# State sums turned through VectorE blocks and DRAM instead of TensorE, and the keys' quad issued next to the features' quad

## The chip, the cores and the metric

The kernel runs on one core of a Trainium2 chip. Its time is the device time of one execution in microseconds (us); a kernel's figure is the median of its runs. Besides the timed runs there is one execution under the hardware profiler, and every duration of a single instruction below comes from that one.

The engines are called as in the profile: PE is TensorE (PEld are its weight loads), DVE is VectorE, ACT is ScalarE, POOL is GpSimd, and SP is the engine that issues the DMAs. Every engine takes its instructions in the order in which they are written, and waits on semaphores for the others.

## The reference: linear attention with running sums, then a small mixture of experts

The input x is 2 x 2048 tokens of 256 channels, in float32. Cut to what matters here:

```python
h = layernorm(x) * (1 + ca) + sa
q, k, v = split(h @ W_attn + b_attn)                 # 16 heads of 16
phi(x) = exp(x @ omega - 0.5 * sum(x * x)) / sqrt(128)   # 128 features per head
S = cumsum(phi_k[..., :, None] * v[..., None, :])    # state: 128 x 16 per head
Z = cumsum(phi_k)                                    # 128 per head
y = (phi_q . S) / (phi_q . Z + 1e-6)
x = x + ga * (y @ W_proj + b_proj)
h = layernorm(x) * (1 + cb) + sb
x = x + gb * moe(h)          # 4 experts, the best 2 of a softmax; base 256 -> 1024 -> 256 and low rank of 4
```

The cumulative sums run over all 2048 tokens of a batch entry.

## The kernel before

**Blocks and steps.** The 4096 tokens are cut into 8 blocks `i` of 512 tokens (blocks 0 to 3 are the first batch entry). The 16 heads form 4 groups `g` of 4 heads, and the 512 tokens form 4 chunks `t` of 128, taken in two pairs `u`. One block therefore has 8 steps `k`, one for each (g, u): step k handles the pair (k // 2, k % 2). The main loop goes over 8 x 8 steps, n = 8 i + k.

**The attention part of one step.** Within a chunk, `scores` (L496) multiplies key and query features into two PSUM banks `pa`, and `masks` (L507, DVE) copies them to SBUF under a causal mask as `am`. Across chunks, the sums S and Z travel as a state: `increments` (L522) forms the chunk's addition, transposed as (heads and values) x features, in the first half of one PSUM bank `py_bank`, and DVE adds it to the running sum `ST` (L535). `turn_sums` (L542) turns two sums with two TensorE transposes, again in `py_bank`, and ACT copies them to SBUF as `S` (L548; DVE in a few early pairs). `outputs` multiplies `am` with the values (L562) and the features with the entering state S (L565), both into the second half of `py_bank`; ACT copies that to `y` (L571), and after each second pair SP stores y (L575).

**Features.** A "quad" is four matmuls with 32 rows each, one for every head of a group, which lie in four row groups of the PE array and run side by side. `features` (L452) is the quad for one side (queries or keys) of one group, followed by four exponentials on ACT (L463). `token_keys` (L478) is the second quad of the keys, with tokens on the partitions, followed by four exponentials (L483). `reload` (L420) loads the inputs of the features from DRAM.

**Dense work.** Each step begins with a share of the dense work (`dense`), so that PE has something to do while the others finish: in even steps query/key projections of the next block (L372), and besides these at k = 0 the turning of the normalized input (L337) and a part of `finish` (L776), at k = 2 `finish` and `project` (L619), at k = 4 `channels2`, `router` (L645), `choose` (some 25 small DVE instructions, L668 to L706) and `finish`, at k = 6 the values (L433). Odd steps hold a "unit" of the hidden layer: `hidden` (L740), then `first` (four low-rank matmuls L725 as a quad, and ACT's ReLU), and after `outputs` `second` (another quad L725, DVE's L767, POOL's L768). Block 1 has units only at k = 5 and 7, block 0 none. The attention part uses the banks `pa` and `py_bank`; all else shares five banks `mm`. In a step with a unit, three of the four features matmuls borrow `py_bank` and `pa` ("spare").

**Order.** `keep_written_order` fixes the order of the instructions on each engine to that in which the program was written; nothing is moved by a scheduler. One step is written in this order: `dense`, `turn_sums`, `first`, `token_keys` of the next group (even k), then for the next pair `increments`, `scores`, `masks` (the first two swapped in odd steps without a unit), then `outputs` of this pair, `second`, `features`, `load_more` (weights, in the first 13 steps), `amid` (at k = 0 the inverse of the denominators: L597 on DVE, then the store L599 and two loads L602 on SP; at k = 1 the division, L611; then `reload`), and `behind` (loads of x at k = 1). Dependencies on a PSUM bank are kept for the tile as a whole: in the profile `outputs` (L562, second half of `py_bank`) waits for DVE's sums (L535, which read the first half).

Of the kernel before, what the change touches and what calls it, by code (L numbers as in the profile page):

```python
# [9 lines left out]
FP = mybir.dt.float32  # L10
# [22 lines left out]
def kernel(  # L33
# [479 lines left out]
    def increments(i, g, u):  # L513

        kt = turned[i, g]
        for e in range(2):
            t = 2 * u + e
            if not carried(i, t):
                continue
            for j in range(HG):  # L520
                v0 = (t * NH + g * HG + j) * DV
                nc.tensor.matmul(  # L522
                    py_bank[j * HW : (j + 1) * HW, e * P : (e + 1) * P],
                    st[i]["vs"][:, v0 : v0 + HW], kt[:, j, t, :], start=True, stop=True,
                )
        for e in range(2):
            t = 2 * u + e
            if not carried(i, t):
                continue
            new = work.tile([P, M], FP, tag=f"ST{g}", name=f"ST{i}_{g}{t}")  # L530
            ps = py_bank[:, e * P : (e + 1) * P]
            if i % NBLK == 0 and t == 0:
                nc.vector.tensor_copy(new, ps)
            else:
                nc.vector.tensor_add(new, ps, S[g])  # L535
            S[g] = sums[i, g, t] = new

    def turn_sums(i, g, u):

        n = sum(carried(i, 2 * u + e) for e in range(2))  # L540
        for e in range(n):
            nc.tensor.transpose(  # L542
                py_bank[:, e * P : (e + 1) * P], sums.pop((i, g, 2 * u + e)), ident
            )
        s2 = work.tile([P, 2, P], FP, tag=f"S{g}", name=f"S{i}_{g}{u}")
        short = (i == 0 and (g, u) != (3, 0)) or (i == 1 and (g, u) in ((0, 0), (0, 1), (1, 1)))
        copy = nc.vector.tensor_copy if short else nc.scalar.copy
        copy(s2[:, 0:n].rearrange("p e d -> p (e d)"), py_bank[:, 0 : n * P])  # L548
        for e in range(n):
            state[i * NT + 2 * u + e + 1, g] = s2[:, e]  # L550

    def outputs(i, g, u):

# [2 lines left out]
        for e in range(2):  # L556
            t = 2 * u + e
            am, s0 = staged.pop((i, g, t)), state.pop((i * NT + t, g), None)
            py = bank[:, (2 + e) * P : (3 + e) * P]
            for j in range(HG):  # L560
                v = st[i]["v"][:, t, g * HG + j, :]
                nc.tensor.matmul(py[rows[j], :], v, am[:, j, :], start=True, stop=s0 is None)  # L562
            if s0 is not None:
                for j in range(HG):
                    nc.tensor.matmul(  # L565
                        py[rows[j], :], s0[:, rows[j]], phi[i, g, 0, j][:, t * P : (t + 1) * P],
                        start=False, stop=True,
                    )
        if u == 0:
# [368 lines left out]
    for i in range(N):  # L938
        for k in range(PAIRS):
# [2 lines left out]
            turn_sums(*pair_at(n))  # L942
            if unit_at(i, k):
                first(*unit_at(i, k))
            if k % 2 == 0 and n + 2 < TOTAL:
                token_keys(*pair_at(n + 2)[:2])
            if n + 1 < TOTAL:
                steps = [increments, scores]
                if k % 2 and not unit_at(i, k):
                    steps.reverse()  # L950
                for step in steps + [masks]:
                    step(*pair_at(n + 1))
# [3 lines left out]
                second(*unit)  # L956
            gi, gg, side = quad_at(n + 3)
            if gi < N:
                spare = [py_bank] + pa if unit else ()
                exponentials(*features(gi, gg, side, spare))  # L960
            load_more(i * PAIRS + k)
            amid(i, k)
            behind(i, k)

# [91 lines left out]
```

## Time and profile before

| what | before |
|---|---|
| median of 3 runs | 741.91 us (740.5 to 750.78) |
| profiled execution, its own time | 742.97 us |
| its span on the core | 741.2 us |
| granted TensorE clock | 0.998 |
| PE busy | 713.5 us (96%) |
| DVE, ACT, POOL busy | 377.5, 341.4, 150.5 us |
| queue that SP issues, share of 16 DMA engines | 29.8% |

The busy time of an engine is the sum over the stretches in which it worked; PE's ends are modelled, so that a busy PE may still be waiting for weights or for its array to empty. A timeline row gives the start, the time from the first start to the last end, the engine, the line, the operation, the tiles (written <- read), the shape, how often, and in brackets the idle time of the engine ahead of it with what ended it.

### The profile page before, as it was taken

What the parts mean: (1) busy time and instruction counts of PE and PEld (TensorE: products, weight loads), DVE (VectorE), ACT (ScalarE), POOL (GpSimd) and SP (SyncE); (2) the same over time, 40 slices, a digit from 0 to 9 for tenths busy, and PEclk for the clock granted to TensorE, in tenths of its full rate; (3) what the DMA queues carried; (4) which work ended last, traced back from release to release, by engine and by line L of the source; (5) the groups of instructions that cost most, each with busy time, mean ns of one, the idle gap of its engine ahead of it and who ended that gap; (6) DMA issues with size and microseconds to landing.
All of it is one profiled execution on the core that took longest, in us unless ns stands there. A gap on an engine that the chain in (4) does not pass through costs nothing.

```text
span 741.2 us, 25787 instructions
## 1 busy us (share of the span) xinstructions
PE 713.5 (96%) x11350; PEld 538.2 (73%) x11350; DVE 377.5 (51%) x1030; ACT 341.4 (46%) x678; POOL 150.5 (20%) x193
## 2 busy tenths in 40 slices
PE   7899898899999999999999999999999999999998
PEld 5466665677777778777777777777787777787776
DVE  5744757454664545564564546644555436522532
ACT  1556454555454554545454554445545554431020
POOL 2101403032321311131120312122101212114022
PEclk9999999999999999999999999999999999999999
DMA  5446456423412242332412243223313322011100
GB/s 149 144 120 183 132 155 178 144 73 99 136 58 88 76 142 63 101 88 89 145 35 89 69 133 101 73 74 90 116 45 101 88 64 85 19 56 47 49 24 29
DMA packets 47664, 69.51 MB, mean 94 GB/s; under 512 B 8320, under 2 KB 21824, under 8 KB 47552
## 3 DMA queue, kind: packets, MB, share of 16 engines
q1 hardware_dynamic: 45936, 66.81, 29.8%
q8 instruction: 89, 1.46, 0.8%
q10 hardware_dynamic: 1616, 1.05, 0.5%
q14 instruction: 23, 0.19, 0.1%
HBM read 38.20 MB, written 29.64 MB: 92 GB/s over the span
## 4 chain that ended last, share of the span: by engine, by line
PE 88%; DVE 6%; ACT 3%; DMA 2%; issue 1%; POOL 0%; SPq 0%; DVEq 0%
PE ph L740 15%; PE pf L776 12%; PE pa L496 8%; PE pq L372 7%; PE pp L452 7%; PE ph L725 5%; PE py_bank L522 4%; PE pk L478 4%; PE py_bank L562 4%; PE po L619 4%; PE py_bank L565 3%; PE pv L433 3%; ACT phi L463 2%; PE pf L799 2%; PE py_bank L542 2%; DMA inv<-rdr 1%
## 5 line engine op out<-in xcount | busy, mean ns | idle before, releaser
L768 POOL TENSOR_TENSOR g<-g,r 128x256 f32<-128x256 f32 x128 | 94.5, 771 | 419.8 <-DVE g L767 419.8
L463 ACT ACTIVATE phi<-pp,lnm 128x512 f32<-128x512 f32 x184 | 113.4, 688 | 52.7 <-PE pp L452 52.7
L740 PE MATMUL ph<-h,wi_sb 128*128 128x256 f32 x480 | 111.6, 386 | 0.0
L740 PEld LDWEIGHTS ph<-h,wi_sb 128*128 128x128 f32 x480 | 87.5, 189 | 32.4 <-ACT y L571 19.0
L776 PE MATMUL pf<-wo_g,g 128*128 128x256 f32 x448 | 103.3, 381 | 0.0
L776 PEld LDWEIGHTS pf<-wo_g,g 128*128 128x128 f32 x448 | 83.3, 190 | 17.0 <-issue 4.9
L535 DVE TENSOR_TENSOR ST<-py_bank,ST 128x128 f32<-128x128 f32 x112 | 32.6, 291 | 122.3 <-PE py_bank L522 94.3
L507 DVE TENSOR_TENSOR am<-pa,causal 128x512 f32<-128x512 f32 x128 | 82.8, 686 | 23.5 <-PE pa L496 22.6
L483 ACT ACTIVATE kt<-pk,lnm 128x512 f32<-128x512 f32 x128 | 77.6, 690 | 23.7 <-PE pk L478 23.7
L496 PE MATMUL pa<-phi,phi 128*32 128x64 f32 (+3 forms) x4096 | 86.3, 234 | 1.6 <-ACT phi L463 0.8
L496 PEld LDWEIGHTS pa<-phi,phi 128*32 128x32 f32 x4096 | 82.4, 110 | 4.3 <-ACT phi L463 3.3
L548 ACT COPY S<-py_bank 128x256 f32<-128x256 f32 (+1 forms) x54 | 19.2, 356 | 115.3 <-PE py_bank L542 115.3
L452 PE MATMUL pp<-f,om 32*128 32x512 f32 x368 | 70.2, 632 | 0.0
L372 PE MATMUL pq<-hT,w_sb 128*128 128x512 f32 x128 | 62.0, 608 | 2.6 <-DVE hT L340 1.6
L784 DVE SCALAR_TENSOR_TENSOR xt<-pf,wt,xt 128x256 f32<-128x256 f32 x32 | 15.4, 482 | 89.6 <-PE pf L776 78.5
L562 PE MATMUL py_bank<-am,v 128*17 128x128 f32 x1024 | 51.3, 273 | 9.1 <-DVE ST L535 8.0
L571 ACT COPY y<-py_bank 128x256 f32<-128x256 f32 x64 | 23.9, 373 | 62.8 <-PE py_bank L565 54.5
L767 DVE SCALAR_TENSOR_TENSOR g<-ph,rho 128x256 f32<-128x256 f32 x120 | 42.5, 417 | 19.8 <-PE ph L725 14.7
L565 PE MATMUL py_bank<-phi,S 128*17 128x128 f32 x960 | 49.5, 273 | 0.0
L372 PEld LDWEIGHTS pq<-hT,w_sb 128*128 128x128 f32 x128 | 22.2, 189 | 32.3 <-issue 15.9
L754 ACT ACTIVATE r<-ph 128x256 f32<-128x256 f32 x120 | 36.6, 389 | 18.4 <-PE ph L725 14.9
L725 PE MATMUL ph<-lT,lb_sb 16*128 16x256 f32 (+1 forms) x480 | 43.5, 425 | 0.7 <-ACT lT L719 0.7
(148 smaller groups left out, 936.1 us busy)
## 6 DMA issues: line engine op xcount, KB each, us to landing
qd<-qs SPq DMA_DIRECT2D x64, 256.0 KB
f<-qd SPq DMA_DIRECT2D x62, 256.0 KB
ydr<-y SPq DMA_DIRECT2D x32, 256.0 KB
num<-ydr SPq DMA_DIRECT2D x16, 256.0 KB
inv<-rdr SPq DMA_DIRECT2D x16, 256.0 KB
xt<-in_x_dram SPq DMA_DIRECT2D x8, 256.0 KB
xt<-in_x_dram SPq DMA_DIRECT2D x32, 64.0 KB
wo_g<-in_woT_dram SPq DMA_DIRECT2D x4, 512.0 KB
```

Of the source, the lines that this page charges most:

```text
L372: nc.tensor.matmul(pq, w_sb[:, k, n * P : (n + 1) * P], s["hT"][:, k, :], start=(k == 0), stop=(k == KC - 1),)
L452: nc.tensor.matmul(pp, om[rs, :], f[rs, :], start=True, stop=True, tile_position=(2 * DH * j, 0))
L463: nc.scalar.activation(ph, pps[j], AF.Exp, bias=lnm)
L483: nc.scalar.activation(kt[:, j].rearrange("p t m -> p (t m)"), banks[j], AF.Exp, bias=lnm)
L496: nc.tensor.matmul(pa[e][c * CG : (c + 1) * CG, j * P + q0 : j * P + q1], k[j][:, t0 + c * CG : t0 + (c + 1) * CG], q[j][:, t0 + q0 : t0 + ...
L507: nc.vector.tensor_mul(am, pa[e][:].rearrange("p (h q) -> p h q", h=HG), causal[:, e, :].unsqueeze(1).to_broadcast([P, HG, P]),)
L562: nc.tensor.matmul(py[rows[j], :], v, am[:, j, :], start=True, stop=s0 is None)
L565: nc.tensor.matmul(py[rows[j], :], s0[:, rows[j]], phi[i, g, 0, j][:, t * P : (t + 1) * P], start=False, stop=True,)
L725: nc.tensor.matmul(ph, lb_sb[rs, (f0 + j) * P : (f0 + j + 1) * P], s["lT"][rs, ts], start=False, stop=True, skip_group_check=True, tile_po ...
L740: nc.tensor.matmul(ph, wi_sb[:, k, f * P : (f + 1) * P], s["h2"][:, k, ts], start=(k == 0), stop=False, skip_group_check=True,)
L768: nc.gpsimd.tensor_add(g, g, r[j // 2][:, j % 2, :])
L776: nc.tensor.matmul(po, s["g"][f][:, t * P : (t + 1) * P], wo_g[i // NBLK][:, f, :], start=(f == 0), stop=(f == NF - 1), skip_group_check=True,
```

## The change

- In blocks 1 to 7 the sums are no longer turned by PE and copied by ACT. Behind the additions, and ahead of the masks, DVE turns each entering sum in 32x32 blocks (L546 of the changed kernel); SP stores the result to DRAM (`sd`) and, at the end of the step, loads it with four DMAs of 32 partitions into `S`, in an order that completes the transposition. `outputs` of the next step waits for these loads. The loads stand in SP's queue behind `load_more` and ahead of `amid`.
- Block 0 still turns on PE, but only the sums that enter (12 transposes remain of 120), and in the step that uses them.
- In an even step whose next step has a unit ("late": 25 steps with a keys' quad), `token_keys` moves from ahead of `increments` to behind `outputs`, right ahead of `features`, which then borrows `py_bank` and `pa` there too.
- The swapped order of `increments` and `scores` stays in block 0 alone.

```diff
--- before.py
+++ after.py
@@ -523,31 +523,67 @@
                     py_bank[j * HW : (j + 1) * HW, e * P : (e + 1) * P],
                     st[i]["vs"][:, v0 : v0 + HW], kt[:, j, t, :], start=True, stop=True,
                 )
+        sums[i, g, u] = []
         for e in range(2):
             t = 2 * u + e
+            if g in S:
+                sums[i, g, u].append((e, S[g]))
             if not carried(i, t):
+                S.pop(g)
                 continue
-            new = work.tile([P, M], FP, tag=f"ST{g}", name=f"ST{i}_{g}{t}")
+            new = work.tile([P, M], FP, tag=f"ST{g}", name=f"ST{i}_{g}{t}", bufs=3)
             ps = py_bank[:, e * P : (e + 1) * P]
-            if i % NBLK == 0 and t == 0:
+            if g in S:
+                nc.vector.tensor_add(new, ps, S[g])
+            else:
                 nc.vector.tensor_copy(new, ps)
-            else:
-                nc.vector.tensor_add(new, ps, S[g])
-            S[g] = sums[i, g, t] = new
+            S[g] = new
+        if i:
+            entering = sums.pop((i, g, u))
+            es = [e for e, _ in entering]
+            st_ = work.tile([P, 4, 2, CG], FP, tag="sT", name=f"sT{i}_{g}{u}")
+            for e, sum_ in entering:
+                nc.vector.transpose(
+                    st_[:, :, e, :], sum_[:].rearrange("p (m k) -> p m k", k=CG)
+                )
+            sd = dram.tile([HG, CG, 4, 2 * CG], FP, tag="sd", name=f"sd{i}_{g}{u}", bufs=3)
+            part = slice(es[0] * CG, 2 * CG)
+            nc.sync.dma_start(
+                sd[:].rearrange("j m b x -> (j m) b x")[:, :, part],
+                st_[:].rearrange("p b e d -> p b (e d)")[:, :, part],
+            )
+            sums[i, g, u] = (es, sd, part)
+
+    def load_state(i, g, u):
+
+        if not i:
+            return
+        es, sd, part = sums.pop((i, g, u))
+        s2 = work.tile([P, HG, 2, HW], FP, tag="S", name=f"S{i}_{g}{u}")
+        for b in range(4):
+            nc.sync.dma_start(
+                s2[b * CG : (b + 1) * CG].rearrange("m j e d -> m j (e d)")[:, :, part],
+                sd[:, :, b, part].rearrange("j m x -> m j x"),
+            )
+        for e in es:
+            state[i * NT + 2 * u + e, g] = s2[:, :, e]
 
     def turn_sums(i, g, u):
 
-        n = sum(carried(i, 2 * u + e) for e in range(2))
-        for e in range(n):
-            nc.tensor.transpose(
-                py_bank[:, e * P : (e + 1) * P], sums.pop((i, g, 2 * u + e)), ident
-            )
-        s2 = work.tile([P, 2, P], FP, tag=f"S{g}", name=f"S{i}_{g}{u}")
-        short = (i == 0 and (g, u) != (3, 0)) or (i == 1 and (g, u) in ((0, 0), (0, 1), (1, 1)))
-        copy = nc.vector.tensor_copy if short else nc.scalar.copy
-        copy(s2[:, 0:n].rearrange("p e d -> p (e d)"), py_bank[:, 0 : n * P])
-        for e in range(n):
-            state[i * NT + 2 * u + e + 1, g] = s2[:, e]
+        if i:
+            return
+        entering = sums.pop((i, g, u))
+        n = len(entering)
+        for e, sum_ in entering:
+            nc.tensor.transpose(py_bank[:, e * P : (e + 1) * P], sum_, ident)
+        s2 = work.tile([P, HG, 2, HW], FP, tag="S", name=f"S{i}_{g}{u}")
+        copy = nc.scalar.copy if (g, u) == (3, 0) else nc.vector.tensor_copy
+        copy(
+            s2[:, :, 2 - n : 2].rearrange("p j e d -> p e j d"),
+            py_bank[:, (2 - n) * P : 2 * P].rearrange("p (e j d) -> p e j d", j=HG, d=HW),
+        )
+        for e, _ in entering:
+            state[i * NT + 2 * u + e, g] = s2[:, :, e]
 
     def outputs(i, g, u):
 
@@ -563,7 +599,7 @@
             if s0 is not None:
                 for j in range(HG):
                     nc.tensor.matmul(
-                        py[rows[j], :], s0[:, rows[j]], phi[i, g, 0, j][:, t * P : (t + 1) * P],
+                        py[rows[j], :], s0[:, j, 0:DV], phi[i, g, 0, j][:, t * P : (t + 1) * P],
                         start=False, stop=True,
                     )
         if u == 0:
@@ -942,11 +978,12 @@
             turn_sums(*pair_at(n))
             if unit_at(i, k):
                 first(*unit_at(i, k))
-            if k % 2 == 0 and n + 2 < TOTAL:
+            late = k % 2 == 0 and unit_at(i, k + 1)
+            if k % 2 == 0 and n + 2 < TOTAL and not late:
                 token_keys(*pair_at(n + 2)[:2])
             if n + 1 < TOTAL:
                 steps = [increments, scores]
-                if k % 2 and not unit_at(i, k):
+                if k % 2 and i == 0:
                     steps.reverse()
                 for step in steps + [masks]:
                     step(*pair_at(n + 1))
@@ -956,9 +993,13 @@
                 second(*unit)
             gi, gg, side = quad_at(n + 3)
             if gi < N:
-                spare = [py_bank] + pa if unit else ()
+                if late and n + 2 < TOTAL:
+                    token_keys(*pair_at(n + 2)[:2])
+                spare = [py_bank] + pa if unit or late else ()
                 exponentials(*features(gi, gg, side, spare))
             load_more(i * PAIRS + k)
+            if n + 1 < TOTAL:
+                load_state(*pair_at(n + 1))
             amid(i, k)
             behind(i, k)
 
```

## The prediction

> **What bounds the kernel now.** I read the shares of busy time first, then the chain of work that ended last, then PE's waits, then the timeline of single steps. The first two say that PE sets the time:
>
> ```profile
> PE 713.5 (96%) x11350; PEld 538.2 (73%) x11350; DVE 377.5 (51%) x1030; ACT 341.4 (46%) x678; POOL 150.5 (20%) x193
> ...
> PE 88%; DVE 6%; ACT 3%; DMA 2%; issue 1%; POOL 0%; SPq 0%; DVEq 0%
> ...
> PE py_bank L562 <- DVE ST L535: 8.0, 9, 2.3
> PE po L619 <- DVE num L611: 3.0, 3, 1.4
> ```
>
> The last two lines are from PE's waits (total us, times, longest). They are small, but they name who is next: `outputs` waits for DVE's sums. So a removed PE instruction is worth its pitch on PE, as long as DVE keeps ahead. Step k = 2 of block 5 shows by how much it does:
>
> ```profile
> 455.07 0.38 PE L542 MATMUL py_bank<-ident,ST 128*128 128x128 f32 x2
> 455.38 1.17 PE L478 MATMUL pk<-om,f 32*128 32x128 f32 x32
> 456.48 0.64 PE L522 MATMUL py_bank<-kt,v 128*32 128x128 f32 x16
> 456.81 0.17 DVE L301 TENSOR_SCALAR rstdf<-mvf 128x4 f32<-128x4 f32 x1
> 457.26 0.62 DVE L535 TENSOR_TENSOR ST<-py_bank,ST 128x128 f32<-128x128 f32 x2 [0.29 <-ACT kt L483]
> 458.06 0.41 PE L562 MATMUL py_bank<-am,v 128*17 128x128 f32 x8
> 459.06 1.14 PE L452 MATMUL pp<-f,om 32*128 32x512 f32 x8
> ```
>
> Call D the end of the dense work (455.07). Increments start at D+1.41, outputs at D+2.99, features at D+3.99. DVE is busy with `project`'s sums and statistics until D+1.91, and its additions start at D+2.19, 0.28 us later, as soon as increments allow.
>
> **Part 1, transposes off PE.** Two transposes hold PE for 455.07 to 455.38, 0.31 us, part of which is the change to the quads' row groups that stays. Near the end of the trace a unit stands without them: hidden starts at 673.88, L725 at 677.53, 3.65 us; with two transposes it is 3.56 + 0.31 = 3.87. So two are worth 0.22, one 0.107. 120 - 12 = 108 go; all on the path, that would be -11.6 us. ACT's 54 copies (356 ns) go too, worth nothing on an engine at 46% that no step waits for there.
>
> **Part 2, quads side by side.** The keys' quad occupies 1.10 us (455.38 to 456.48), though 32 matmuls of 128 columns in four row groups need 32 x 0.107 / 4 = 0.86: 0.24 goes to emptying the row groups. Where L725 is followed by features it takes 0.53 instead of 0.64, so about 0.1 of that remains between quads. The moved quad then costs 0.95, 0.15 less, in 25 steps: -3.8 us. ACT must run eight exponentials in a row (0.605 each, by rows of 2.42 for four) behind it; from about 3.6 to 8.45 us after increments start. The next step's scores need the last one at 9.27, its hidden needs the first bank at 4.5 and gets it at 4.25. That covers it with little to spare; were it gone, each 0.1 us would cost 2.5 us in 25 steps.
>
> **Part 3, what is late next.** With transposes and quad gone from ahead of increments, these start at D+0.09 and outputs could start at D+1.67. At k = 0 and 6, DVE is free at D+0.69 and D+0.63: no wait; features then start at 1.67 + 1.0 + 0.95 = D+3.62, a gain of 0.37. At k = 2 DVE's additions can't start before D+1.93; they take 0.62, and outputs start at D+2.6. The moved quad now stands behind this wait and not under it: features at D+4.57, a loss of 0.58. At k = 4 `choose` and L784 hold DVE until D+1.82: features at D+4.43, loss 0.44. In blocks 1 and 7 k = 4 waits for DVE already (outputs at D+5.57 and D+3.81); there the whole 0.95 is added. Blocks 3 and 7 have one addition less and are some 0.1 better. Sum over even steps: k = 0 and 6, 12 x -0.37 and one of -0.2 = -4.6; k = 2 (blocks 2 to 7), 4 x 0.58 + 2 x 0.45 = +3.2; k = 4, 4 x 0.44 + 0.33 + 2 x 0.95 = +4.0. That is **+2.6**.
>
> In odd steps only transposes go: 18 x 0.22 + 8 x 0.107 = **-4.8**.
>
> **Part 4, DVE's turns.** They stand between the additions and the masks, which in odd steps end at 3.06 us after increments start, while the borrowed bank is written from 3.15 on. The trace has this operation at 212 ns for 128x32 (L694), and 407 for another of 128x256 (L327); by elements about 0.3 for 128x128. Four of L327 take 1.37, so starts follow at 0.79 of a duration. Two turns behind the second addition (started at 1.11) would free DVE for the masks at about 1.84 instead of 1.77: 0.07 in 20 odd steps, **+1.4**. Without any overlap it would be 2.12, and 0.33 x 20 = 6.6 us. I take the first, as independent DVE instructions do overlap in the rows; ends 0 and 6.6. [...]
>
> **Part 5, the road through DRAM.** The nearest store is 128 x 256 bytes:
>
> ```profile
> 352.58 0.32 SPq L599 DMA_DIRECT2D rdr<-den  x1
> 354.07 1.28 SPq L602 DMA_DIRECT2D inv<-rdr  x2
> ```
>
> L602 waits for its landing: 1.49 us after the issue began. The state's store has 128 KB, I add 0.35. The nearest load (den, 128 runs of 256 bytes) is issued in 0.59 and its last packet ended 1.8 us after its start, 2.75 in a crowded stretch. Turned at 1.9, stored, first load at 3.75, fourth at 5.7, landed at 7.5 us after increments started. Its reader L565 comes 10.4 us after in the shortest full step pair, some 11.6 where Part 3 adds a wait. Hidden, with 3 us to spare. If that cover goes, each us costs 26 us over the odd steps. A 256-byte packet took 17.5 ns in the trace, so 512 per pair keep 16 engines busy 0.6 us. SP's own queue: behind the loads stand `reload` (needed a step later) and at k = 0 the inverse's store and loads, 2.7 us later than now; they land near D+13 when DVE's division is due at D+13.7, and PE has 2 more us. [...]
>
> Block 1 has no cover at k = 0 to 3. There SP is late already:
>
> ```profile
> 107.40 1.28 SPq L602 DMA_DIRECT2D inv<-rdr  x2
> ...
> 114.38 3.29 PE L619 MATMUL po<-wp_g,num 128*128 128x256 f32 x14 [1.37 <-DVE num L611]
> ```
>
> Ahead of L602 come eight weight loads (99.42 to 105.35), and then, new, four state loads (2.6 us). I find the inverse's second load at 111.2 instead of 108.08, of which 0.9 is lost in other waits: project starts 2.2 us later (1.2 to 3.1; earlier gains of this block vanish in that wait). At k = 3 the sums' loads, behind weights, miss L565 by 1.3; the undone swap returns the 0.74 that L562 waited. **+2.8** (1 to 6).
>
> **Sum**: 2.6 - 4.8 + 1.4 + 2.8 and -0.2 in block 0 = +1.8 (in block 0 four transposes go, half of them under waits). Against the profiled execution's own 742.97 us that is 744.8; the median of the runs shown is 1.06 lower, so **743.7 us**, no change that a measurement could tell (2% is about what it can).
>
> **Rivals.** (a) *Slower: the state comes late everywhere.* Mechanism: `outputs` waits at L565 for four loads. It decides from a landing 10.4 us after increments. If each issue took 1.4 us (one of the lb_sb weight loads did, 1.39, in a wait) and the landing den's 2.75: 1.9 + 1.85 + 3 x 1.4 + 2.75 = 10.7, and about 11.4 if a reload of 256 KB is still moving; over by 1 us in 26 odd steps: +26 on the sum, 770. For: five more DMAs a step on one queue. Against: SP waits most of the time. 0.13.
> (b) *Faster: DVE doesn't hold up k = 2 and 4.* If outputs no longer waited for the additions, those 13 steps would gain 0.37 each like the others: 1.8 - 7.2 - 4.8 = -10, 733. Against it: nine waits on L535, and the same bank is shared. 0.2.
> (c) *DVE becomes the bound of odd steps*: no overlap of turns, +5.2, 749. 0.12.
> The forecast itself 0.5; the rest (0.05) is unnamed.
>
> **Numbers.** The forecast's own bounds are 737 to 751 (turns 0 to 6.6, block 1 1 to 6, quads 2 to 6). With (b) and (c), and their sizes' spread, 731 to 757; out stay (a) and the unnamed. Faster than 727: 0.06 (b with block 1 free). Slower than 757: 0.16. Within: 0.78.
>
> **What would show it.** The L542 group falls to 12, PE's busy time by about 15 us; PE's waits grow a line "L562's successor <- DVE ST" of about 11 waits of 0.8 to 0.9 at k = 2 and 4; no wait of the state matmuls on a DMA outside block 1; the masks of odd steps start near 1.84 us after increments; project in block 1 starts near 116.5. I am wrong if PE waits for the state's loads in most steps, if k = 2 and 4 show no wait, or if exponentials delay scores in odd steps.

## The result, and the profile after

The changed kernel took 751.4 us (median of 20 runs, 747.21 to 755.36) against 744.77 us for the kernel before (20 runs beside them): a ratio of 1.0084, 95% interval 1.0058 to 1.0110. That is 6.6 us slower, clearly so, and less than the 2% taken as the bound of a difference. Its profiled execution took 747.21 us, as little as the shortest of the 20 runs, with a span of 745.4 us and a granted clock of 0.986 (before: 742.97, 741.2 and 0.998). The medians lie above the profiled executions, by 4.2 us here and 1.8 us before; only the profiled ones have a trace, so every place named below is a place in those. Medians are of all runs, ratios leave out the few runs in a slower, disturbed state, and the one experiment whose profiled execution fell in that state has a time below and no stretches.

The page of the kernel after, its shares of busy time and the chain that ended last:

```profile
PE 705.5 (95%) x11242; PEld 526.4 (71%) x11242; DVE 390.7 (52%) x1135; ACT 319.8 (43%) x625; POOL 148.7 (20%) x193
...
PE 81%; DVE 11%; DMA 3%; ACT 3%; issue 1%; SPq 0%; POOL 0%; DVEq 0%
```

PE lost the 108 transposes and is still the bound, but DVE's share of the chain has gone from 6% to 11%. PE's waits (total us, times, longest) say where:

```profile
PE py_bank L598 <- DVE ST L537: 15.1, 17, 3.9
PE py_bank L601 <- DMA S<-sd: 7.0, 2, 5.1
...
PE po L655 <- DVE num L647: 2.6, 3, 1.1
```

L598 is the first half of `outputs` (L562 before), L601 the half that reads the state (L565 before). The first line was 8.0 us in 9 waits before. The second is new: two waits in this execution, both in block 1.

**A step with k = 2.** The same step of block 5 as shown before, from the timeline of the kernel after:

```profile
463.42 0.64 PE L522 MATMUL py_bank<-kt,v 128*32 128x128 f32 x16
...
465.07 0.17 DVE L301 TENSOR_SCALAR rstdf<-mvf 128x4 f32<-128x4 f32 x1
465.15 0.62 DVE L537 TENSOR_TENSOR ST<-py_bank,ST 128x128 f32<-128x128 f32 x2
...
465.68 0.49 DVE L546 STREAM_TRANSPOSE sT<-ST 128x128 f32<-128x128 f32 x2
...
465.82 0.41 PE L598 MATMUL py_bank<-am,v 128*17 128x128 f32 x8 [0.62 <-DVE ST L537]
...
466.83 1.17 PE L478 MATMUL pk<-om,f 32*128 32x128 f32 x32
...
467.83 0.59 PE L452 MATMUL pp<-f,om 32*128 32x512 f32 x1
```

DVE is busy with `project`'s statistics up to L301, its additions start 1.73 us after increments, and PE stands still for 0.62 us ahead of `outputs`. The moved quad (L478) comes behind this wait and no longer covers it. Features start 4.41 us after increments; the prediction has them at D+4.57 with increments at D+0.09, that is 4.48.

**Stretch by stretch.** PE's increments cut the trace into stretches: stretch k goes from the increments of pair k to those of pair k+1, so it holds the end of step k-1 and the dense work of step k. Moving the quad takes time out of the even stretches and puts it into the odd ones. Medians over blocks 2 to 6, in us, worked out from the L522 rows:

| stretch | 0 + 1 | 2 + 3 | 4 + 5 | 6 + 7 | block |
|---|---|---|---|---|---|
| before | 11.72 + 8.16 | 14.34 + 8.16 | 12.58 + 12.05 | 10.89 + 8.16 | 86.1 |
| after | 10.44 + 8.83 | 13.06 + 9.67 | 11.31 + 13.47 | 9.56 + 8.83 | 85.2 |
| change | -0.61 | +0.23 | +0.15 | -0.66 | -0.9 |
| predicted | -0.52 | +0.43 | +0.29 | -0.52 | -0.3 |

The predicted row puts Parts 1 to 4 together: the even step's change, then -0.22 for the odd step's transposes and +0.07 for its masks. So a full block became faster, as the even steps k = 0 and 6 promise. The loss is in one place:

| | block 1 | blocks 2 to 6, each | block 7 | end | span |
|---|---|---|---|---|---|
| before | 75.9 | 86.1, 84.7, 85.4, 87.3, 86.1 | 68.8 | 76.7 | 741.2 |
| after | 86.9 | 85.2, 84.2, 84.3, 85.2, 85.2 | 69.2 | 74.8 | 745.4 |
| change | +11.0 | -5.5 | +0.3 | -2.0 | +4.2 |

(Each figure is rounded by itself. Block 7 has seven stretches; the end is what follows the last increments. 0.4 is lost ahead of block 0. Up to 1.7 of the end's gain is a stretch of half clock, 3.4 us long, that only the profile before has, and 1.1 of block 5's a single wait there.)

**Block 1.** Windows of the kernel after, one for each stretch k = 2 to 5 of block 1 (length, busy time of each engine, granted clock, DMA share, GB/s):

```profile
106.40:122.80 16.40, 13.48 (x177) 8.79 (x176) 7.74 (x22) 3.42 (x6) 1.63 (x2) 0.81 0.48 147
122.80:127.50 4.70, 4.70 (x131) 3.35 (x127) 4.22 (x13) 3.79 (x7) 1.91 (x2) 1.00 0.72 203
127.50:142.30 14.80, 9.67 (x199) 5.90 (x200) 5.84 (x13) 4.23 (x8) 2.48 (x2) 0.77 0.63 182
142.30:159.00 16.70, 12.12 (x201) 8.78 (x189) 6.41 (x31) 6.51 (x12) 0.00 (x0) 0.80 0.39 112
```

and the same four before:

```profile
107.10:118.90 11.80, 9.69 (x122) 6.30 (x112) 7.11 (x18) 3.80 (x7) 0.90 (x1) 1.00 0.72 213
118.90:126.10 7.20, 6.68 (x198) 5.04 (x198) 5.00 (x12) 5.22 (x9) 3.39 (x4) 1.00 0.55 166
126.10:135.00 8.90, 7.95 (x176) 4.74 (x167) 6.46 (x17) 3.88 (x8) 1.75 (x2) 1.00 0.39 122
135.00:147.00 12.00, 9.00 (x154) 6.66 (x150) 4.86 (x23) 6.18 (x11) 0.00 (x0) 1.00 0.41 133
```

Three of the four stretches are 4.6 to 5.9 us longer, the second is 2.5 us shorter, and in the three the granted clock is around 0.8, where it was 1.00 before. So there are two things: PE waits, and while its clock is at half, behind such waits, its matmuls take nearly twice as long. Both can be seen in the timeline of the third of them:

```profile
124.39 0.60 SPq L390 DMA_DIRECT2D qd<-qs  x1
...
125.09 0.60 SPq L391 DMA_DIRECT2D qd<-qs  x1
...
125.78 0.58 SPq L551 DMA_DIRECT2D sd<-sT  x1
...
126.41 1.62 SPq L232 DMA_DIRECT2D wo_g<-in_woT_dram  x1
...
129.29 0.41 PE L598 MATMUL py_bank<-am,v 128*17 128x128 f32 x8
...
131.32 2.08 SPq L564 DMA_DIRECT2D S<-sd  x4
...
134.81 0.63 PE L601 MATMUL py_bank<-phi,S 128*17 128x128 f32 x8 [5.12 <-DMA S<-sd]
...
136.23 2.09 PE L452 MATMUL pp<-f,om 32*128 32x512 f32 x8
```

SP issues the store of the turned sums at 125.78, behind x (five loads from 121.94 on) and two stores of 256 KB (L390, L391), and can issue the loads only at 131.32, when the store has landed: 5.5 us, where the kernel before shows 1.49 for a store of 32 KB with nothing ahead of it. PE waits 5.12 us, and its features then take 2.09 us instead of the 1.14 of the steps at full clock.

### The profile page after: what moved, and what is told of

It reads as the page before. It is cut to its first block, busy times and chain, and to the rows that moved or that the text cites. A ratio compares the mean times of both kernels' runs of the same rounds, so it can differ in the third digit from the quotient of the medians.

```text
span 745.4 us, 26121 instructions
## 1 busy us (share of the span) xinstructions
PE 705.5 (95%) x11242; PEld 526.4 (71%) x11242; DVE 390.7 (52%) x1135; ACT 319.8 (43%) x625; POOL 148.7 (20%) x193
## 4 chain that ended last, share of the span: by engine, by line
PE 81%; DVE 11%; DMA 3%; ACT 3%; issue 1%; SPq 0%; POOL 0%; DVEq 0%
PE ph L776 15%; PE pf L812 10%; PE pq L372 7%; PE pa L496 7%; PE pp L452 6%; PE ph L761 5%; PE pk L478 5%; PE py_bank L598 4%; PE py_bank L522 4%; PE py_bank L601 3%; PE pv L433 3%; PE po L655 2%; PE pf L835 2%; ACT phi L463 2%; DMA inv<-rdr 1%
## 5 line engine op out<-in xcount | busy, mean ns | idle before, releaser
L804 POOL TENSOR_TENSOR g<-g,r 128x256 f32<-128x256 f32 x128 | 92.8, 757 | 418.9 <-DVE g L803 418.9
L537 DVE TENSOR_TENSOR ST<-py_bank,ST 128x128 f32<-128x128 f32 x112 | 32.6, 291 | 115.1 <-PE py_bank L522 99.5
L496 PE MATMUL pa<-phi,phi 128*32 128x96 f32 (+3 forms) x4096 | 87.2, 235 | 1.7 <-ACT phi L463 0.8
L483 ACT ACTIVATE kt<-pk,lnm 128x512 f32<-128x512 f32 x128 | 77.5, 688 | 25.8 <-PE pk L478 25.8
L463 ACT ACTIVATE phi<-pp,lnm 128x512 f32<-128x512 f32 x109 | 70.5, 692 | 38.9 <-PE pp L452 38.9
L598 PE MATMUL py_bank<-am,v 128*17 128x128 f32 x1024 | 52.1, 277 | 15.1 <-DVE ST L537 15.1
L372 PE MATMUL pq<-hT,w_sb 128*128 128x512 f32 x128 | 63.6, 621 | 2.3 <-DVE hT L340 1.2
L463 ACT ACTIVATE phi<-pa,lnm 128x512 f32<-128x512 f32 x98 | 62.9, 710 | 0.0
L601 PE MATMUL py_bank<-phi,S 128*17 128x128 f32 x960 | 50.6, 278 | 7.0 <-DMA S<-sd 7.0
L452 PE MATMUL pa<-f,om 32*128 32x512 f32 x196 | 54.3, 623 | 0.0
L452 PE MATMUL py_bank<-f,om 32*128 32x512 f32 x98 | 53.2, 623 | 0.0
```

The source lines that it names most:

```text
L372: nc.tensor.matmul(pq, w_sb[:, k, n * P : (n + 1) * P], s["hT"][:, k, :], start=(k == 0), stop=(k == KC - 1),)
L452: nc.tensor.matmul(pp, om[rs, :], f[rs, :], start=True, stop=True, tile_position=(2 * DH * j, 0))
L463: nc.scalar.activation(ph, pps[j], AF.Exp, bias=lnm)
L483: nc.scalar.activation(kt[:, j].rearrange("p t m -> p (t m)"), banks[j], AF.Exp, bias=lnm)
L496: nc.tensor.matmul(pa[e][c * CG : (c + 1) * CG, j * P + q0 : j * P + q1], k[j][:, t0 + c * CG : t0 + (c + 1) * CG], q[j][:, t0 + q0 : t0 + ...
L601: nc.tensor.matmul(py[rows[j], :], s0[:, j, 0:DV], phi[i, g, 0, j][:, t * P : (t + 1) * P], start=False, stop=True,)
```

## Experiments on the two parts of the change

**The quad alone** (the kernel before with the moved quad, whose features borrow the same banks as in the change; the sums are left alone):

```diff
-            if k % 2 == 0 and n + 2 < TOTAL:
+            late = k % 2 == 0 and unit_at(i, k + 1)
+            if k % 2 == 0 and n + 2 < TOTAL and not late:
...
+                if late and n + 2 < TOTAL:
+                    token_keys(*pair_at(n + 2)[:2])
```

> Kernel before with the keys' quad moved as in the change, sums still turned by PE. Theory A (behind outputs the quad no longer fills PE's wait for DVE at k = 2 and 4): k = 0 and 6 gain 0.15 us each (12 times), k = 2 and 4 lose 0.58 and 0.44 to 0.95 as in the changed kernel: 5 us slower, ratio 1.007. Rival B (the quad next to a quad saves 0.15 us in 25 steps, nothing waits): 4 us faster, ratio 0.995.

Measured: 751.76 us, ratio 1.0115 (1.0068 to 1.0163). Theory A's side, and by more than it said. A full block takes 87.4 us instead of 86.1, and the reason is another one than DVE: all four pairs of stretches are 0.3 to 0.4 us longer, those of k = 0 and 6 too, which theory A let gain. PE's waits of this run:

```profile
PE py_bank L522 <- ACT S L548: 12.0, 25, 1.0
PE py_bank L562 <- DVE ST L535: 8.2, 8, 2.4
```

In the kernel before, the quad stood between the transposes and the increments, and ACT's copy of the turned sums out of `py_bank` ran under it. With the quad gone the copy lies open, 0.46 us in 24 of 25 steps; less the 0.15 to 0.2 that a moved quad gains, that is the 0.3. So the two parts of the change belong together: the quad may move only because the transposes and this copy go.

**The state alone** (the kernel after, with the quad left in its place):

```diff
-            late = k % 2 == 0 and unit_at(i, k + 1)
+            late = False
```

> Changed kernel with the keys' quad back ahead of the increments: only the state's road is changed. Theory A: 0.22 us per step gained in blocks 2 to 7, some 10 to 11 us, given back by block 1: 6 to 7 us below the changed kernel, ratio to before 0.998 to 1.002; at k = 2 and 4 of blocks 2 to 6 no wait of outputs for DVE's sums. Rival B (the road through DRAM costs time everywhere): no faster than the changed kernel, ratio 1.008.

Measured: 744.32 us, ratio 0.9994 (0.9964 to 1.0025), as theory A says. Its stretches are 11.50 + 7.94, 14.12 + 7.94, 12.37 + 11.83 and 10.67 + 7.94, in sum 84.3 against 86.1: 1.74 us less for the 16 transposes of a block, 0.109 for each. Block 1 takes 83.0 us (75.9 before) and eats up most of it. PE's wait for the state is larger here than in the kernel after:

```profile
PE py_bank L601 <- DMA S<-sd: 11.8, 5, 4.9
```

Three of the five waits, 3.1 us in all, lie outside block 1, in front of pair 1 of block 3 and pair 3 of blocks 4 and 5.

**The quad only where DVE is free** (the kernel after, quad moved at k = 0 and 6 alone):

```diff
-            late = k % 2 == 0 and unit_at(i, k + 1)
+            late = k in (0, 6) and unit_at(i, k + 1)
```

> Changed kernel with the quad moved only at k = 0 and 6, and left ahead of the increments at k = 2 and 4. Theory A: the waits of outputs for DVE's sums go from 17 to about 4, each step k = 2 and 4 gains 0.6 to 0.95 us: 8 to 10 us below the changed kernel, ratio to before 0.995 to 0.998. Rival B (the moved quad gains everywhere): 1 to 2 us above the changed kernel, ratio 1.010.

Measured: 741.13 us, ratio 0.9955 (0.9928 to 0.9982), as theory A says and faster than both kernels. The stretches are 10.44 + 8.83, 14.16 + 7.94, 12.37 + 11.83 and 9.57 + 8.83. Against the run before this one the moved quad gains 0.17 at k = 0 and 0.21 at k = 6; against the kernel after, leaving it in place gains 0.63 at k = 2 and 0.58 at k = 4, and 3.3 in stretches 4 and 5 of block 1. The waits on DVE's additions fall from 17 to 6 (6.4 us).

## Experiments on block 1

**Weights behind the state's loads** (`load_more` after `load_state`; at k = 0 of block 1, where it issues the eight loads of `lb_sb`, at the end of the step):

```diff
-            load_more(i * PAIRS + k)
             if n + 1 < TOTAL:
                 load_state(*pair_at(n + 1))
+            if n != 8:
+                load_more(n)
             amid(i, k)
             behind(i, k)
+            if n == 8:
+                load_more(n)
```

> Changed kernel with one edit in SP's queue: the state's loads go ahead of the weight loads of the same step, and the eight low-rank weight loads of step (1,0) go to the end of that step. Theory A (the loss sits in block 1, where the state's loads and the inverse stand behind weight loads, and PE's idle time there also halves its granted clock): 5 to 8 us below the changed kernel, ratio to before 0.998 to 1.002, the 1.9 us wait at step (1,1) gone, the 5.1 us wait at (1,3) shorter but not gone, because its store still shares the DMA engines with x and the projections. Rival B (the state's traffic slows all blocks alike): at most 2 us below, ratio 1.006 or more.

Measured: 756.71 us, ratio 1.0157 (1.0129 to 1.0186): 5 us slower than the kernel after, where theory A wanted 5 to 8 faster. Of the waits for the state, the one of 1.86 us is down to 0.20 and the one of 5.12 to 3.91, as theory A said, yet block 1 takes 93.6 us. Its timeline, SP's issues and DVE's division:

```profile
101.93 0.33 SPq L551 DMA_DIRECT2D sd<-sT  x1
...
105.81 1.75 SPq L564 DMA_DIRECT2D S<-sd  x4
...
110.17 1.27 SPq L638 DMA_DIRECT2D inv<-rdr  x2
...
111.99 6.56 SPq L228 DMA_DIRECT2D lb_sb<-in_bT_dram  x8
...
117.78 0.69 DVE L647 TENSOR_TENSOR num<-num,inv 128x512 f32<-128x512 f32 x1 [3.06 <-DMA lb_sb<-in_bT_dram]
118.66 0.36 SPq L551 DMA_DIRECT2D sd<-sT  x1
```

With the weights out of the way SP stands idle for 3.5 us until the store has landed (3.9 after its issue), the inverse is issued only 1.5 us earlier than in the kernel after (110.17 against 111.69), and its second half is used at 117.78, no earlier than there (117.71). The weights now delay the next store instead (118.66 against 113.57), `project` waits 2.98 us for the division, and in stretch 4 a new wait of 3.28 us stands ahead of L337, for DVE's gate (L271), which itself waits for weights (`wo_g`) that are loaded later here. So it is not the place of the eight weight loads alone: whatever stands behind the state's loads on this queue waits with them for the store's landing, and in neither of the two orders tried is nothing late in block 1. The weights on another engine's queue were not tried.

**Block 1 turned on PE** (the road through DRAM from block 2 on), and the same with the quad only at k = 0 and 6 (the same condition in `load_state` and `turn_sums`):

```diff
-        if i:
+        if i > 1:
             entering = sums.pop((i, g, u))
```

> Changed kernel, but block 1 turns its sums on PE like block 0, so that no state goes through DRAM before block 2. Theory A (block 1 holds the whole loss): block 1 as short as in the kernel before, no clock dips there, 9 to 11 us below the changed kernel, ratio to before 0.994 to 0.997. Rival B (loss spread over the blocks): 1 to 2 us below, ratio 1.006.

> Both: block 1 on PE, and the quad moved only at k = 0 and 6. Theory A: the two gains add, 17 to 19 us below the changed kernel, ratio to before 0.983 to 0.987. Rival B (the two edits buy the same time): no lower than the better one alone, ratio 0.995.

Measured: 747.85 us, ratio 1.0069 (1.0035 to 1.0102), for the first; 741.39 us, 0.9951 (0.9913 to 0.9990), for the second. Block 1 took 79.6 and 81.0 us, less than the 86.9 and 82.9 of the same kernels with the road, but not the 75.9 of before, and both ratios are those of theory B. PE's waits of the first name the reason:

```profile
PE py_bank L522 <- DVE S L581: 7.1, 4, 4.9
```

The edit had DVE copy the turned sums, and at k = 4 that copy stands behind `choose`'s small instructions. That is a wait of the experiment's own making, so it was taken out in two further runs, both with the quad at k = 0 and 6. First ACT makes the copy:

```diff
-        copy = nc.scalar.copy if (g, u) == (3, 0) else nc.vector.tensor_copy
+        late_act = (g, u) == (3, 0) if i == 0 else (g, u) not in ((0, 0), (0, 1), (1, 1))
+        copy = nc.scalar.copy if late_act else nc.vector.tensor_copy
```

> The kernel after with two parts undone: the keys' quad moves only at k = 0 and 6, and in block 1 too the sums are turned on PE, with ACT making the copy except in the first two and the fourth pair (the kernel before had it so). The same with DVE making the copies gave 741.4 us; its copy stood behind choose, and increments waited 4.9 us for it. Theory A: block 1 is dear because of the road of its sums, first through DRAM, then through a late copy. Then the wait of increments on the copy goes, block 1 takes 75 to 78 us (81.0 with DVE's copies, 75.9 in the kernel before), no stretch of half clock of 6.8 us is left in it, and the ratio to before is 0.986 to 0.991. Theory B: something else of the change makes block 1 dear (the moved quads at k = 6, the order of increments and scores). Then block 1 stays at 80 or more and the ratio at 0.995.

Measured: 740.21 us, ratio 0.9925 (0.9881 to 0.9969): between the theories, with both in the interval; there are no stretches to settle it. Then the order of increments and scores is swapped back as well, which makes block 1 nearly that of the kernel before:

```diff
-                if k % 2 and i == 0:
+                if k % 2 and not unit_at(i, k):
                     steps.reverse()
```

> The kernel of the run before (keys' quad moved at k = 0 and 6 alone, block 1's sums turned on PE with ACT's copies, 740.2 us, ratio 0.9925) with the third part of block 1 undone: increments and scores are swapped again in its odd steps without a unit, as in the kernel before. Block 1 then differs from the kernel before only in the entering sums' own time of turning and in one moved quad (k = 6). Theory A: all that block 1 lost hung on its sums (the road through DRAM, the late copy, the order made for it). Then block 1 takes 74.5 to 77 us (75.9 in before, 86.9 in after, 82.9 with only the quad put back), PE never waits over 2.5 us in it, no stretch of half clock of 6.8 us lies in it, and the ratio is 0.984 to 0.991. Theory B: turning an entering sum in the step that uses it is itself late, whoever copies. Then block 1 stays at 79 or more with a wait of over 3 us on that copy or behind it, and the ratio is 0.992 to 0.997.

Measured: 738.69 us, ratio 0.9919 (0.9879 to 0.9958), the lowest median of this study, 4.8 us below the kernel before in the same batch (743.48). Block 1 takes 77.5 us, the longest wait in it is 2.33 us, and the granted clock of the profiled execution is 1.000. Theory A's bounds (0.991 and 77) are missed by a little; the ratio's interval holds both theories. What decides is block 1: of theory B nothing is there, no 79 us, no wait of over 3 us on the copy. PE's waits:

```profile
PE py_bank L599 <- DVE ST L537: 7.8, 8, 2.3
PE py_bank L602 <- DMA S<-sd: 5.1, 4, 2.1
```

The second line shows what is left of the road's cost: among them a wait of 2.1 us each in blocks 2 and 3, which the profile of the kernel after does not have.

**PE kept busy in block 1's waits** (the kernel after, with transposes of the identity that nobody reads ahead of `outputs` in three steps):

```diff
+            fill = {(1, 1): 14, (1, 3): 44, (1, 4): 33}.get((i, k), 0)
+            if fill:
+                warm = mm_tile(f"warm{i}_{k}")
+                for m in range(fill):
+                    nc.tensor.transpose(warm[:, (m % 4) * P : (m % 4 + 1) * P], ident, ident)
             outputs(*pair_at(n))
```

> Changed kernel with transposes of the identity that nothing reads, written ahead of outputs at steps (1,1), (1,3) and (1,4): 14, 44 and 33 of them, about 1.5, 4.7 and 3.5 us of PE work where PE waits 1.9, 5.1 and 3.9 us. Theory A (PE's idle time halves the granted clock for windows of 3.4 us, which lengthens the matmuls behind each wait): the dips of the clock at 133 and 147 us go, 3 to 5 us below the changed kernel. Rival B (only the wait itself costs): 0 to 1 us above.

Measured: 747.02 us, ratio 1.0055 (1.0026 to 1.0084); 4.4 us below the kernel after by medians, which is theory A's size, but with intervals that overlap, and the profiled execution is 2.2 us longer. So the total settles nothing, and the stretches must. The windows of stretches 4 and 5 of block 1:

```profile
130.50:143.40 12.90, 12.68 (x245) 9.69 (x248) 5.89 (x13) 4.20 (x8) 2.52 (x2) 1.00 0.49 151
143.40:158.10 14.70, 13.54 (x231) 10.92 (x223) 6.44 (x31) 6.52 (x12) 0.00 (x0) 1.00 0.43 130
```

They are 12.9 and 14.7 us long instead of 14.8 and 16.7, at a clock of 1.00 instead of 0.77 and 0.80. PE gets to the awaited work hardly sooner in the one and later in the other: in stretch 4 its state matmuls start 7.10 us after increments instead of 7.33 (the state itself comes 2.3 us earlier here, but the filling holds PE), in stretch 5 its `outputs` start at 6.28 instead of 5.69.

```profile
132.38 5.02 PE L994 MATMUL warm<-ident 128*128 128x128 f32 x44
...
137.56 0.40 PE L601 MATMUL py_bank<-phi,S 128*17 128x128 f32 x8
```

From there to the next increments it takes 5.8 us instead of 7.5, and 8.4 instead of 11.0. So half clock cost 1.7 and 2.6 us there, beside the waits. In stretch 2 the filling did harm: `project` waited 2.95 us for the division and the stretch became 3.2 us longer, so block 1 as a whole gained only 0.3.

## Experiments on the state's road through DRAM

**Four more loads** (the kernel after; from block 2 on, four loads into an unread tile ahead of the four real ones):

```diff
+        if i > 1:
+            spare_s = work.tile([P, HG, 2, HW], FP, tag="S2", name=f"more{i}_{g}{u}")
+            for b in range(4):
+                nc.sync.dma_start(
+                    spare_s[b * CG : (b + 1) * CG].rearrange("m j e d -> m j (e d)")[:, :, part],
+                    sd[:, :, b, part].rearrange("j m x -> m j x"),
+                )
```

> Changed kernel with four more loads of the state, into a tile that nothing reads, ahead of the real four, in blocks 2 to 7: each state lands some 2 us later and SP issues nine DMAs a step for it. Theory A (the state has 3 us to spare in these blocks): 0 to 2 us above the changed kernel. Rival B (the state is just in time): 2 us in each of 26 odd steps, up to 50 us above.

Measured: 805.32 us, ratio 1.0841 (1.0790 to 1.0891): 54 us above the kernel after, on rival B's side. At k = 0 of block 4, the timeline of the kernel after:

```profile
356.44 0.60 SPq L390 DMA_DIRECT2D qd<-qs  x1
357.49 0.59 SPq L391 DMA_DIRECT2D qd<-qs  x1
359.10 0.34 SPq L551 DMA_DIRECT2D sd<-sT  x1
...
364.00 1.75 SPq L564 DMA_DIRECT2D S<-sd  x4
...
367.69 0.41 PE L601 MATMUL py_bank<-phi,S 128*17 128x128 f32 x8
```

and that of this run:

```profile
378.89 0.60 SPq L390 DMA_DIRECT2D qd<-qs  x1
379.59 0.60 SPq L391 DMA_DIRECT2D qd<-qs  x1
380.39 0.34 SPq L551 DMA_DIRECT2D sd<-sT  x1
...
386.71 1.75 SPq L565 DMA_DIRECT2D more<-sd  x4
388.56 3.20 SPq L571 DMA_DIRECT2D S<-sd  x4
...
393.21 0.41 PE L608 MATMUL py_bank<-phi,S 128*17 128x128 f32 x8 [4.04 <-DMA S<-sd]
```

In the kernel after the loads are issued 4.9 us after the store, and the last issue ends 1.9 us before PE uses the data. From the packets of 256 bytes in the trace one can say when the state's last one ended. Over blocks 2 to 6, where the trace has the packets, in us after increments:

| pair | store issued | landing took | last packet of S | its reader | spare |
|---|---|---|---|---|---|
| k = 0 | 1.84 | 1.35 | 7.1 | 12.2 | 4.2 to 5.7 |
| k = 1 | 1.82 | 4.5 | 9.1 | 10.6 | 1.0 to 2.7 |
| k = 3 | 2.78 | 3.8 | 10.3 | 11.5 | 0.5 to 3.0 |
| k = 6 | 1.84 | 2.8 | 7.9 | 11.4 | 3.2 to 3.7 |
| k = 7 | 1.84 | 2.2 | 7.5 | 10.6 | 2.5 to 3.7 |

Landing took, spare: median and span from the trace's packets. Pair 1's store is issued right behind L390 and L391, 512 KB; pair 3's behind x and another two of these. Where PE does wait for the state in this run, its last packet ended 0.43 to 0.5 us before PE went on in all but two cases, so in some blocks the kernel after has next to nothing to spare at pair 3 and half a microsecond at pair 1. The other runs bear that out: in eight further profiles with the road through DRAM, all nine waits of over 1 us for the state outside block 1 (up to 2.2 us) stand ahead of pair 1 or 3, and three of these profiles run the kernel after's own program from block 2 on. That the profile of the kernel after has none is its good fortune.

"3 us to spare" is thereby refuted for pairs 1 and 3, and holds about, with 2 us or more, for the others. PE waits at pair 7 too in this run, because the state comes there 4.5 us later (12.0 instead of 7.5), more than the 2 us that were expected of four loads.

**Two more loads** (the same with two):

> The kernel after with two more loads of the state ahead of the four that are needed (into a tile that nobody reads), from block 2 on; four of them cost 54 us. By the packets of the profile after, the state's last packet ends 0.5 to 1.9 us before its reader starts at k = 0, 0.5 to 4 at k = 2 and 3 or more in the other steps, of which 0.17 is needed. Two issues of 0.47 take 0.95. Theory A (spare of under 1 us in a few steps, and each wait makes the next store later): some 5 waits of 0.1 to 0.7 us, 2 to 8 us in all, ratio 1.011 to 1.019. Theory B (3 us to spare, and the four loads failed by filling the queue): 0 to 1 us, ratio 1.008 to 1.010. Theory C (the cost goes with the number of loads): half of 54, ratio 1.040 to 1.050.

Measured: 771.89 us, ratio 1.0369 (1.0272 to 1.0467): 20 us above the kernel after, beyond theory A's 2 to 8 and below theory C's half. PE's wait for the state is now

```profile
PE py_bank L608 <- DMA S<-sd: 22.0, 11, 4.3
```

instead of 7.0. Theory A counted the issues alone (0.95 us), but for pair 1 the last packet comes at 11.2 us after increments instead of 9.1. Of these 2.1 us the issues are 0.95; 0.9 more lies in the store's landing (5.3 us instead of 4.5) and the rest between the last issue and the last packet. The extra loads also lengthen the queue that the next store stands in: pair 2's store is issued at 6.2 us instead of 2.8. The four-load run shows the whole loop: the wait for S grew by 37.6 us in 15 more waits, and 41.0 us of half clock lie in blocks 2 to 7, where the kernel after has none.

**The store on another queue** (the kernel after, the state's store issued by ACT):

```diff
-            nc.sync.dma_start(
+            nc.scalar.dma_start(
                 sd[:].rearrange("j m b x -> (j m) b x")[:, :, part],
```

> The kernel after, with the store of the turned sums issued by ACT instead of SP; the loads stay with SP. In the profile after, the store's last packet ended 1.35 us after its issue where nothing was ahead of it, and 2.9 to 5.6 us after it in the steps in which two stores of 256 KB (L390, L391) had been issued by SP just before. Theory A: it waits its turn in SP's queue. Then it lands 1.3 to 2 us after its issue in all steps, the first load of S at k = 0 is issued 3.5 to 4.5 us after increments start (6.0 to 6.7 in after), the wait for S in block 1 falls from 5.1 to under 3, and the time is 2 to 5 us below after (ratio 1.000 to 1.006). Theory B: what is in flight delays it on whichever queue it is. Then the loads are issued where they were, and the time is that of after or more (1.007 to 1.015), since ACT waits for DVE's turns ahead of the issue.

Measured: 750.98 us, ratio 1.0086 (1.0048 to 1.0123), the kernel after's. Both theories hold in part. For pairs 3 and 5 the landing fell to 1.35 and 1.36 us (3.8 and 3.1), so there the store had stood in SP's queue. For pair 1 it stayed at 4.2 (4.5), for pairs 4 and 6 at 3.2 and 2.6 (3.0 and 2.8): there it is late on whichever queue it is, and what the trace shows beside it is traffic. In the kernel after, over blocks 2 to 6, the 16 DMA engines were busy 0.53 to 0.59 of the time while pair 1's store landed, and 0.29 while pair 0's did in the 1.35 us of blocks 2 and 5. In block 1 the wait of 5.12 us became 2.29, and `project` waited 3.6 us for the division instead of 1.06. Pairs 3 and 5 gained 2.5 and 1.8 us of landing, more than the store's issue takes (0.34 us).

## Why the prediction came out, and which steps did not

The forecast was 743.7 us and "no change that a measurement could tell"; the median is 751.4, inside the range and on its slow side. Of the 7.7 us between them, 2.9 lie in the base (741.9 by three runs, 744.8 by twenty); the change itself was forecast at +1.8 and measured at +6.6, or +4.2 in the profiled executions. Point by point:

- **What bounds the kernel** (PE, DVE next): right. The chain and the 17 waits on L537 show it.
- **Part 1, 0.107 for a transpose:** right, 0.109 in the run with the state alone. PE's busy time fell by 8 us and not by the 15 announced, since matmuls at half clock are longer (block 1 alone went from 67.6 to 72.5 us busy, with fewer matmuls); in the last variant, with full clock throughout and 92 transposes gone, it is 700.8, 12.7 less.
- **Part 2, a moved quad gains 0.15:** right, 0.17 and 0.21. That the 0.24 goes to emptying the row groups was the author's reading; the trace before shows that it lies at the quad's two ends, where the second four matmuls start 0.21 us behind the first four and L522 0.22 behind the last four, with 0.11 from four to four elsewhere. The exponentials delayed no scores: the wait of scores on them is 0.8 us, in two waits, as in the run with the quad left in its place.
- **Part 3, k = 2 and 4 lose and k = 0 and 6 gain:** right in sign everywhere, and 0.1 to 0.2 us too slow for each, as the table of stretches shows, 0.03 to 0.07 of it by Part 4. The announced waits are there, ten of 0.5 to 0.6 us at k = 2 and 4 of blocks 2 to 7 and one of 2.14, where some 11 of 0.8 to 0.9 were forecast. Over five and a half blocks the kernel is by this 3 us faster than predicted. Rival (b) is thereby refuted (its 733 should read 732, since its -10 counts from 741.9), and the quad's own run showed the cover that the prediction had not named: it also hid ACT's copy.
- **Part 4, turns cost 0.07 in odd steps:** right for the turns, dear for the steps. The turns take 0.49 us for two and masks start 1.85 us after increments (predicted 1.84), but the last borrowed bank is written at 3.19 instead of 3.15, so a step pays 0.04 at k = 1, 3 and 7 and mostly nothing at k = 5: some 0.6 us in place of 1.4. The prediction's own rows left 0.09 between the masks' end (3.06) and that bank (3.15), and it did not count them. Rival (c) is refuted.
- **Part 5, "Hidden, with 3 us to spare":** the outcome held outside block 1, the size did not. The landing at 7.5 us is that of pair 7. The step that failed is the 1.49 us of a store with an empty queue, put in for every step (with 0.35 on top for its 128 KB, an allowance of the author's; at k = 0 of block 5, with nothing ahead, the first load was issued 1.77 us after the store, where the sum of the two is 1.84): behind 512 KB the store took 4.5 us, and pairs 1 and 3 kept 0.5 to 3 us. Rival (a), which was judged by the same price, was closer than 0.13 says; two further loads bring it about at pairs 1 and 3.
- **Block 1, "+2.8 (1 to 6)":** the term that was mis-sized, and it decides the sign. Block 1 lost 11.0 us, of which the prediction gives about 3 (2.8, 0.95 for k = 4, some tenths back). `project` went on 4.1 us later and not 2.2 (118.45 against 114.38); the wait for the sums at k = 3 is 5.12 and not 1.3, by the same landing; one at k = 1 (1.86) was not foreseen; the wait at k = 4 grew to 3.91 from 2.33. And half clock was not in the sum at all: 20.5 us of it in four stretches, three behind these waits and one (105.7) ahead of them. Behind the waits at k = 3 and 4 it cost 4.3 us, by the run with PE kept busy; for the other two, of 3.4 us, the loss is at most 1.7 each, by their length, and both lie ahead of waits for a DMA's data (1.86 and 1.06 us), which cover much of it. What the 11 us hang on is shown by two variants: with the quad left in its place at k = 4 block 1 takes 82.9 us, 4.0 less, where Part 3 had put 0.95 (the wait there stays at 2.46 us, and no half clock follows it); with its sums and their order as before as well it takes 77.5, another 5.4 less; 1.6 remain.

The two errors, 8 us too few in block 1 and some 5 too many elsewhere (3 of them in Parts 3 and 4, 3 in single events of the profile before, less 0.6 ahead of block 1), cancel for the most part in the profiled executions: that the forecast lies as near as it does is luck. In the medians the change costs 2.4 us more than in the profiles. Waits for the state at pairs 1 and 3, which the profile after happens not to have and the three others with the same program from block 2 on have for 0.8 to 1.4 us, may be part of that; it is not shown, and the rest stays open.

## What to carry to other kernels

Price a round trip through DRAM by the traffic ahead of it at each place where it happens, not by a transfer on an empty queue, and then test the spare by delaying the data: here 1 us of more issues a step cost 20 us, most of it at two pairs of eight. A move that is good in some steps can be made in those alone: the wait list names the steps in which the moved work had covered something. And a wait of PE can cost more than its length, because of the clock that follows it (here 1.7 and 2.6 us more behind waits of 5.12 and 3.91); look at the granted clock of the stretch behind the wait.

## What the runs showed of the hardware that was not expected

The granted clock of TensorE went to 0.5 for stretches of 3.4 us or two to four times that (3.41, 3.41, 6.83 and 6.83 in the kernel after), and their starts lie on a grid of 3.41 us (105.7, 112.5, 133.0 and 146.6 us in the kernel after, that is 2, 6 and 4 times 3.41 apart). In thirteen profiles of this case, all after 60 us, PE's idle times were followed by half clock (on in them, or begun in them or within 3.5 us behind them) as often as this:

| PE idle | followed by half clock |
|---|---|
| 3.8 to 5.3 us | 17 of 17 |
| 2.6 to 3.5 us | 11 of 12 |
| 2.0 to 2.6 us | 9 of 26 |
| 0.9 to 1.9 us | 9 of 52 |

Under it the features' eight matmuls took 2.09 us instead of 1.14. Six stretches near 105 us began ahead of any such idle time, during or just behind L240, 16 matmuls of two columns that take 1.95 us at full clock (two of the six are in the table by an idle time that fell into them); in the other seven profiles the same matmuls had no half clock, so what sets it off there stays open. How much idle time it takes these runs do not settle: one of 2.0 to 2.6 us, shorter than a step of the grid, was followed by half clock in 9 of 26 cases, and the 2.33 us in block 1 of the kernel before was not.

The other surprise is the loop through SP's queue: a late load makes the next store late, since both stand in one order (6.2 us after increments instead of 2.8 for pair 2, with two more loads), and the store's landing was longer where more was in flight: in the kernel after 1.35 us at a DMA share of 0.29 (pair 0 of blocks 2 and 5) and 4.5 at 0.53 to 0.56 (pair 1 of blocks 2 to 4), for the same 128 KB.
